# One lot of contractions per step: moving half of a step's y-contraction to the beginning of the next step in a convolution, scan and experts kernel

## The chip, the cores and the metric

One NeuronCore of a Trainium2 chip. The metric is the device time of one launch in microseconds; where several executions are compared, their median is taken. Engine names are those of the profile: PE is the TensorE (matmuls), PEld its weight loads, DVE the VectorE, ACT the ScalarE, POOL the GpSimd, SP the SyncE, which issues most of the DMAs.

## What is computed

Two layers on an input of 8 images, 128 channels, 64 x 64 pixels: a deformable 3 x 3 convolution, then a selective scan over the 4,096 pixels of each image as tokens, then a mixture of eight experts with the best two chosen. The scan is what matters here:

```python
deltaA = jnp.exp(jnp.einsum('bld,dn->bldn', delta, A))
deltaB = jnp.einsum('bld,bln->bldn', delta, Bv)

def step(state, inp):
    dA_i, dB_i, x_i, C_i = inp
    state = dA_i * state + dB_i * x_i[:, None, :]
    y = jnp.einsum('bdn,bn->bd', state, C_i)
    return (state, y)
```

`d` and `n` both run over 256, so each image has a state of 256 x 256 numbers, and each of the 4,096 steps multiplies it by the exponentials, adds an outer product and contracts it with `C`.

## The kernel before

**The steps.** All eight images advance together. One step takes a token of each. A state lies with `n` on the 128 partitions, in two halves `h`, and `d` along the row. The eight images are four pairs, `PAIRS = ((0, 2), (1, 3), (5, 7), (4, 6))`. Pairs 0 to 2 have their states in SBUF (`ht`), pair 3 in PSUM (`ud`). One step does, for each pair p:

- `product(j, c, lo, p)` (line 999): exponentials `et` times state, into a buffer. For pairs 0 to 2 it runs on POOL, into `mt[(3 * j + p) % 4]` (four buffers for three pairs), and for pair 3 on DVE, into `md[j % 2]`.
- `unit(c, lo, pairs)` (line 982): outer products on PE, for pairs 0 to 2 into `up`, which is one PSUM tile that the three pairs use in turn, for pair 3 into `ud`.
- `add(j, p)` (line 1006): DVE adds product and outer product into the new state, `ht[p]` or `ud`.
- `contract(j, c, lo, pairs)` (line 1013): PE multiplies the *product* by `C` and accumulates in `yp`, 16 matmuls for two pairs. (The outer product's share of y is added later, through `qt`.) Each matmul fills 32 of the array's columns, and four neighbours of the order fill all 128. It reads `mt` or `md`, so that buffer can't be written again before it is done.

Two steps are a chunk `c`. Their exponentials are made a chunk ahead: `decay` (line 952) makes one group of logarithms on PE in one of three PSUM banks, and ACT takes the exponential into the other of two `et` buffers. A chunk has 19 such groups.

**The order.** The program of every engine is written out by hand in `scan_block`: a step has 12 slots, and what is issued at a slot stands there. At slot 0 a decay, the contraction of pairs (1, 2) of the step before and `product` 2; at slot 3 `unit` of pairs 0 and 3 and `add` 0; at 5 `add` 3; at 6 `unit` 1 and, in the first step of a chunk, the contraction of pairs (0, 3) of this very step; at 7 `add` 1; at 8 the contraction of (0, 3) in the second step of a chunk; at 9 `unit` 2; at 11 `add` 2. `product` 0 and 1 of a step stand ahead of its slots; that of pair 3 is issued at slot 9 or 11 of the step before. Decays stand at the head of nearly every slot.

The rest (gathers and convolution of the block ahead, its projections, and the experts of the block behind) is fed into the slots by a planner, `Work.step` (line 482). It keeps a load for PE and DVE, which `cost` raises with each piece (5 for a contraction of two pairs, 2 for `unit`, 1 for `decay` on PE; 6 for a large DVE operation). Each slot takes `RATE` off the load, and a thread may issue its next piece only if both loads are below `ROOM`.

Sixteen steps are a block, 32 blocks one body of the loop, and the loop runs eight times. Before it the images are normalised and their table of gather addresses is made (the first 1.8 ms).

Of the kernel before, what the change touches and what calls it, by code (L numbers as in the profile page):

```python
# [46 lines left out]
CH = 2  # L47
# [19 lines left out]


RATE = (3.2, 3.2)
ROOM = (7.0, 9.0)  # L70

PACE = 0.8
AHEAD = 2.0
# [3 lines left out]
def kernel(  # L77
# [392 lines left out]
    def cost(pe=0, dve=0):  # L470
        load[0] += pe
        load[1] += dve
        paced[0] += pe * paced[1]

    class Work:
# [3 lines left out]
        def add(self, gen, at=0):  # L479
            self.threads.append([gen, at])  # L480

        def step(self, slot):
# [5 lines left out]
            for t in list(self.threads):  # L488
                if t[1] <= slot and all(x < r for x, r in zip(load, ROOM)):
                    n = next(t[0], None)  # L490
# [433 lines left out]
    def load_r(k, c):  # L924
        assert ("rows", k) in there
        nc.sync.dma_start(
            out=rt[c % 2],
            in_=rz[k].rearrange("q x -> (q x)")[: KR * NCH * RROW].rearrange(
                "(p c x) -> p c x", p=KR, c=NCH
            )[:, c, :],  # L930
        )

    def load_u(k, c):
        assert ("delta", k) in there and ("b", k) in there
        for p in range(QI // 2):
            nc.sync.dma_start(
                out=uu[c % 2][32 * p : 32 * p + 9].rearrange("r w b l n -> r (w b) (l n)"),
                in_=pr[k].rearrange("i j p w b l n -> p (i j) (w b) (l n)")[
                    p, :, :, CH * DIN * c : CH * DIN * c + CH * DIN
                ],  # L940
            )
# [10 lines left out]
    def decay(c, g):  # L952

        ps = banks.pop(0)
        rv = rt[c % 2].rearrange("p (q g t) -> p q g t", q=GD, t=CT)
        if g < NG - 1:
            fs, n, d0 = 1, GD, P * (g % 2) + GD * (g // 2)
        else:
            fs, n, d0 = 2, P - NA * GD, NA * GD
        m = n * CT  # L960
        for h in range(NH):
            for f in range(fs):
                nc.tensor.matmul(  # L963
                    ps[:, m * (NH * f + h) : m * (NH * f + h + 1)].rearrange(
                        "p (q t) -> p q t", q=n
                    ),
                    alhs[:KR, g + f, P * h : P * h + P], rv[:, :n, g + f, :],
                    start=True, stop=True,
                )
        ec = et[c % 2].rearrange("p l b h d -> p h (l b) d")  # L970
        for f in range(fs):
            nc.scalar.activation(  # L972
                ec[:, :, :, P * f + d0 : P * f + d0 + n],
                ps[:, m * f * NH : m * (f + 1) * NH].rearrange(
                    "p (h d t) -> p h t d", h=NH, d=n
                ),
                AF.Exp,
            )
        banks.append(ps)
        cost(1)  # L980

    def unit(c, lo, pairs):

        for h in range(NH):
            for p in pairs:
                for r, b in enumerate(PAIRS[p]):
                    rows = slice(32 * (b // 2), 32 * (b // 2) + 32)
                    nc.tensor.matmul(  # L988
                        (up if p < QP else ud)[:, r, h],
                        uu[c % 2][rows, 0, b % 2, lo, P * h : P * h + P],  # L990
                        uu[c % 2][rows, 1, b % 2, lo, :], start=True, stop=True,
                    )
        cost(2)

    def buf(j, p):

        return mt[(QP * j + p) % 4] if p < QP else md[j % 2]

    def product(j, c, lo, p):
        (nc.gpsimd if p < QP else nc.vector).tensor_tensor(  # L1000
            buf(j, p), et[c % 2][:, lo, PAIRS[p][0] : PAIRS[p][1] + 1 : 2],
            ht[p] if p < QP else ud, ALU.mult,
        )
        cost(0, 0 if p < QP else 6)
# [8 lines left out]
    def contract(j, c, lo, pairs):  # L1013
        l = j % BL
        for h in range(NH):
            for r in range(2):
                for p in pairs:
                    b = PAIRS[p][r]
                    s0 = 32 * (CH * (QI * h + b) + lo) + 31 - (BL * (b % 2) + l)
                    nc.tensor.matmul(  # L1020
                        yp[32 * (b // 2) : 32 * (b // 2) + 32, :DIN],
                        zc[c % 2].rearrange("p s x -> p (s x)")[:, s0 : s0 + 32],
                        buf(j, p)[:, r, h, :],
                        start=(l == 0 and h == 0 and b % 2 == 0),
                        stop=(l == BL - 1 and h == NH - 1 and b % 2 == 1),
                    )
        cost(5)

    def after(k, c, n):

        return ((k + (c + n) // NCH) % 2, (c + n) % NCH)

    last = []

    def scan_block(s, work):

        k = s % 2
        for c in range(NCH):
            for lo in range(CH):
                j0 = CH * c + lo  # L1040
                j = BL * s + j0
                if lo == 0:
                    load_u(*after(k, c, 1))
                    load_r(*after(k, c, 2))
                for p in range(2):
                    product(j, c, lo, p)
                for sl in range(NSLOT):
                    x = NSLOT * lo + sl

                    g = x * NG // (CH * NSLOT - 3)  # L1050
                    if g < NG and (x == 0 or g > (x - 1) * NG // (CH * NSLOT - 3)):
                        decay((c + 1) % NCH, g)
                    nxt = (j + 1, c + (lo + 1) // CH, (lo + 1) % CH)
                    if sl == 0:
                        if last:
                            contract(*last.pop())
                        product(j, c, lo, 2)
                    elif sl == 3:
                        unit(c, lo, (0, 3))
                        add(j, 0)  # L1060
                    elif sl == 5:
                        add(j, 3)
                    elif sl == 6:
                        unit(c, lo, (1,))
                        if lo + 1 < CH:
                            contract(j, c, lo, (0, 3))
                    elif sl == 7:
                        add(j, 1)
                        if lo == 0:
                            copy_c(*after(k, c, 1))  # L1070
                    elif sl == 8 and lo + 1 == CH:

                        contract(j, c, lo, (0, 3))
                    elif sl == 9:
                        if lo + 1 < CH:
                            product(*nxt, 3)
                        unit(c, lo, (2,))
                    elif sl == 11:
                        add(j, 2)
                        if lo + 1 == CH:  # L1080
                            product(*nxt, 3)
                        last.append((j, c, lo, (1, 2)))
                    work(NSLOT * j0 + sl)

    def run(gen):
        for _ in gen:
            pass
        while later:
            run(later.pop(0))

    for b0 in range(0, NB, QI):

        run(conv(b0, 0, 0))
        run(project(0))
        run(conv(b0, BL, 1))
        for p in range(QP):
            nc.vector.memset(ht[p], 0.0)
        nc.vector.memset(ud, 0.0)
        load_r(0, 0)
        load_r(0, 1)  # L1100
        load_u(0, 0)
        copy_c(0, 0)
        for g in range(NG):
            decay(0, g)
        product(0, 0, 0, 3)
        with tc.For_i(0, NBLOCK * BL, BODY * BL) as i0:
            with tc.manual_schedule():
                work = Work()
                load[:] = 0.0, 0.0
                paced[:] = 0.0, 0.0  # L1110
                for s in range(BODY):
                    work.add(project(1 - s % 2))
                    work.add(conv(b0, i0 + BL * (s + 2), (s + 2) % 4), CONV_AT - LOADS)
                    scan_block(s, work.step)
                    assert not [t for t in work.threads]

                    work.threads.insert(
                        0, [behind(b0, i0 + BL * s, s % 2, s % 4), 2]
                    )
                contract(*last.pop())  # L1120
                run(work.threads[0][0])


# [41 lines left out]
```

## Time and profile before

| | |
|---|---|
| median of 3 runs | 38,419.15 us (38,351.94 to 38,429.86) |
| the profiled execution's own time | 37,966.97 us |
| its span, first to last instruction | 37,965.3 us |
| granted TensorE clock, mean | 0.963 |
| loop, first to last product on POOL | 1,777 to 37,929 us |

The parts of a step that the change touches, from the groups of instructions (all lie inside the loop):

| what | engine, count | mean of one |
|---|---|---|
| contraction, L1020, from `mt` | PE, 98,304 | 395 ns |
| contraction, L1020, from `md` | PE, 32,768 | 407 ns |
| decay, L963 | PE, 81,960 | 254 ns |
| outer product into `up`, L988 | PE, 49,152 | 274 ns |
| exponential, L972 | ACT, 40,980 | 519 ns |
| product of pairs 0 to 2, L1000 | POOL, 12,288 | 2,367 ns |
| add into `ht`, L1008 | DVE, 12,288 | 1,218 ns |

Matmuls in different columns of the array run side by side, so a contraction of 16 matmuls takes not 16 x 0.4 us but about 1 us. The busy shares of the page are means over the whole loop. No engine is full, so the reader has to go by waits: who stood still, and for whom.

### The profile page before, as it was taken

The page shows a single profiled execution, that of the slowest core. Times are in us where ns is not written, and L with a number is a line of the kernel's source. Part 1 is how long each engine was busy: PE and PEld are TensorE (multiplying, and loading weights), DVE is VectorE, ACT ScalarE, POOL GpSimd, SP SyncE. Part 2 cuts the span into 40 slices and gives each one's busy share as a digit, 9 for nine tenths or more (in the row PEclk, how much of TensorE's full clock was granted, in tenths as well). Part 3 has the DMA queues.
Part 4 walks back from the last instruction along what each step waited for, and adds up shares of the span by engine and source line. Part 5 has one row for each costly group of instructions (what it writes and reads, how often), then busy time and mean ns, then how long its engine had stood idle before and what let it go on. Part 6 is the DMA issues. An engine that isn't in the chain of part 4 may idle for free. (4 is left out here: it accounts for less than half of the span.)

```text
span 37965.3 us, 852122 instructions
## 1 busy us (share of the span) xinstructions
PE 31439.9 (83%) x324270; PEld 17736.9 (47%) x324270; DVE 27307.6 (72%) x35860; ACT 24040.0 (63%) x62725; POOL 31045.4 (82%) x14691
## 2 busy tenths in 40 slices
PE   3488888888888888888888888888888888888888
PEld 1144444444444444444444444444444444444444
DVE  1277777777777777777777777777777777777777
ACT  0166666666666666666666666666666666666666
POOL 0188888888888888888888888888888888888888
PEclk7799999999999999999999999999999999999999
DMA  3333333333333333333333333333333333333333
GB/s 88 76 103 103 104 105 103 103 106 105 105 102 105 105 103 105 103 104 104 105 102 104 106 105 105 101 106 105 105 104 104 104 103 105 105 103 103 105 105 100
DMA packets 4799916, 3906.86 MB, mean 103 GB/s; under 512 B 3351550, under 2 KB 4378967, under 8 KB 4536023
## 3 DMA queue, kind: packets, MB, share of 16 engines
q1 hardware_dynamic: 4529962, 3182.00, 30.2%
q0 software_dynamic: 185760, 608.85, 5.9%
q10 hardware_dynamic: 80072, 61.51, 0.6%
q8 instruction: 2532, 41.48, 0.5%
q14 instruction: 1590, 13.02, 0.1%
HBM read 3268.71 MB, written 582.10 MB: 101 GB/s over the span
## 5 line engine op out<-in xcount | busy, mean ns | idle before, releaser
L1000 POOL TENSOR_TENSOR mt<-et,ht 128x1024 f32<-128x1024 f32 x12288 | 28725.1, 2367 | 4748.9 <-ACT et L972 3456.5
L972 ACT ACTIVATE et<-bank 128x448 f32<-128x448 f32 (+1 forms) x40980 | 19926.5, 519 | 10802.0 <-PE bank L963 10474.1
L1008 DVE TENSOR_TENSOR ht<-mt,up 128x1024 f32<-128x1024 f32 x12288 | 14968.0, 1218 | 8812.8 <-PE ud L988 5603.9
L963 PE MATMUL bank<-rt,alhs 126*128 126x224 bf16 (+1 forms) x81960 | 12579.9, 254 | 2341.6 <-ACT et L972 2056.9
L963 PEld LDWEIGHTS <-alhs 126*128 126x128 bf16 x81960 | 6874.8, 99 | 7549.5 <-issue 6746.3
L1020 PE MATMUL yp<-mt,zc 128*32 128x256 f32 x98304 | 9099.6, 395 | 0.0
L988 PE MATMUL up<-uu 32*128 32x256 bf16 x49152 | 4993.7, 274 | 1969.9 <-DVE ht L1008 1899.2
L1010 DVE TENSOR_TENSOR ud<-md,ud 128x1024 f32<-128x1024 f32 x4096 | 5004.4, 1222 | 0.0
L1000 DVE TENSOR_TENSOR md<-et,ud 128x1024 f32<-128x1024 f32 x4097 | 4975.1, 1214 | 23.7 <-ACT et L972 23.7
L1020 PEld LDWEIGHTS yp<-mt,zc 128*32 128x32 f32 x98304 | 3411.5, 111 | 2805.6 <-issue 1378.5
L1020 PE MATMUL yp<-md,zc 128*32 128x256 f32 x32768 | 4664.2, 407 | 0.0
L988 PEld LDWEIGHTS <-uu 32*128 32x128 bf16 x65536 | 1786.7, 92 | 5060.7 <-issue 4445.9
L611 PE MATMUL bank<-ident,w 128*128 128x128 f32 x18576 | 3142.5, 292 | 341.4 <-ACT et L972 216.0
L601 ACT ACTIVATE w<-g,rec 128x128 f32<-128x128 f32 x9288 | 3196.2, 404 | 127.2 <-DMA rec<-recs 114.6
L611 PEld LDWEIGHTS bank<-ident,w 128*128 128x128 f32 x18576 | 2429.5, 191 | 1136.1 <-ACT et L972 538.2
L578 POOL DMA_INDIRECT g<-table,rec x2322 | 2261.6, 974 | 500.6 <-issue 228.0
L988 PE MATMUL ud<-uu 32*128 32x256 bf16 x16384 | 1604.4, 272 | 361.5 <-DVE md L1000 342.8
L1020 PEld LDWEIGHTS yp<-md,zc 128*32 128x32 f32 x32768 | 1691.0, 113 | 0.0
L896 ACT ACTIVATE se<-bank,gate 128x128 f32<-128x128 f32 x2048 | 696.2, 367 | 540.2 <-PE bank L889 487.2
L301 POOL MEMSET xpad<- 128x66 f32 x8 | 1.2, 153 | 1232.7 <-POOLq L268 1232.6
L554 PE MATMUL bank<-wconv_sb,vt 128*128 128x128 f32 x4644 | 905.5, 295 | 0.0
L554 PE MATMUL bank<-ident,se 128*128 128x128 f32 x4096 | 820.7, 305 | 0.0
(200 smaller groups left out, 16358.4 us busy)
## 6 DMA issues: line engine op xcount, KB each, us to landing
rt<-rz SPq DMA_DIRECT2D x2050, 1102.5 KB
uu<-pr SPq DMA_DIRECT2D x8196, 36.0 KB
pr<-dpt SPq DMA_DIRECT2D x3084, 48.0 KB
pr<-bpt SPq DMA_DIRECT2D x3084, 48.0 KB
rz<-dst SPq DMA_DIRECT2D x6939, 21.0 KB
g<-table,rec POOLq DMA_INDIRECT x2322, 3.5
rec<-recs SPq DMA_DIRECT2D x2064, 2.8 KB
table<-xtok SPq DMA_DIRECT2D x256, 128.0 KB
```

The costliest lines, as they stand in the source:

```text
L554: nc.tensor.matmul(ps_out, lhs, rhs, start=(i == 0), stop=(i == n - 1))
L578: nc.gpsimd.indirect_dma_start(out=g, out_offset=None, in_=table, in_offset=bass.IndirectOffsetOnAxis(ap=rec.bitcast(I32)[:, j : j + 1], a ...
L601: nc.scalar.activation(ws[j][:, P * q : P * q + P], g[:, P * q : P * q + P], AF.Copy, scale=rec[:, c0 : c0 + 1],)
L611: nc.tensor.matmul(wk[:, :P], w[:, P * q : P * q + P], ident, start=(q == 0), stop=(q == 3),)
L896: nc.scalar.activation(se[:, ex, :], wk[:, P * j : P * j + P], AF.Copy, scale=gate[:, ex : ex + 1],)
L963: nc.tensor.matmul(ps[:, m * (NH * f + h) : m * (NH * f + h + 1)].rearrange("p (q t) -> p q t", q=n), alhs[:KR, g + f, P * h : P * h + P], ...
L972: nc.scalar.activation(ec[:, :, :, P * f + d0 : P * f + d0 + n], ps[:, m * f * NH : m * (f + 1) * NH].rearrange("p (h d t) -> p h t d", h= ...
L988: nc.tensor.matmul((up if p < QP else ud)[:, r, h], uu[c % 2][rows, 0, b % 2, lo, P * h : P * h + P], uu[c % 2][rows, 1, b % 2, lo, :], st ...
L1000: (nc.gpsimd if p < QP else nc.vector).tensor_tensor(buf(j, p), et[c % 2][:, lo, PAIRS[p][0] : PAIRS[p][1] + 1 : 2], ht[p] if p < QP else ...
L1008: nc.vector.tensor_tensor(ht[p], buf(j, p), up, ALU.add)
L1010: nc.vector.tensor_tensor(ud, buf(j, p), ud, ALU.add)
L1020: nc.tensor.matmul(yp[32 * (b // 2) : 32 * (b // 2) + 32, :DIN], zc[c % 2].rearrange("p s x -> p (s x)")[:, s0 : s0 + 32], buf(j, p)[:, r, ...
```

## The change

The contraction of pairs (0, 3) is no longer issued in its own step. It is kept in `last` with that of (1, 2), and both are issued in one lot in the next step, ahead of slot 0 and its decay. They stand behind that step's `product` 0 and ahead of its `product` 1. The latter writes the `mt` buffer that the contraction of pair 0 reads: `(3 * (j + 1) + 1) % 4` equals `(3 * j) % 4`. `ROOM` for PE goes from 7 to 9.

```diff
-ROOM = (7.0, 9.0)
+ROOM = (9.0, 9.0)
...
-                for p in range(2):
-                    product(j, c, lo, p)
+                product(j, c, lo, 0)
+                if last:
+                    for what in last.pop():
+                        contract(*what)
+                product(j, c, lo, 1)
...
                     if sl == 0:
-                        if last:
-                            contract(*last.pop())
                         product(j, c, lo, 2)
...
                     elif sl == 6:
                         unit(c, lo, (1,))
-                        if lo + 1 < CH:
-                            contract(j, c, lo, (0, 3))
...
-                    elif sl == 8 and lo + 1 == CH:
-
-                        contract(j, c, lo, (0, 3))
...
                         if lo + 1 == CH:
                             product(*nxt, 3)
-                        last.append((j, c, lo, (1, 2)))
+                        last.append([(j, c, lo, (0, 3)), (j, c, lo, (1, 2))])
...
-                contract(*last.pop())
+                for what in last.pop():
+                    contract(*what)
```

## The prediction

> **What bounds the kernel now.** First the page, part 1: is one engine full?
>
> ```profile
> PE 31439.9 (83%) x324270; PEld 17736.9 (47%) x324270; DVE 27307.6 (72%) x35860; ACT 24040.0 (63%) x62725; POOL 31045.4 (82%) x14691
> ```
>
> None is. PE and POOL are both near 82%, so the waits have to say who holds whom. The view of waits (engine and line, what it waited for: us in total, times, longest):
>
> ```profile
> ACT et L972 <- PE bank L963: 10474.1, 10831, 14.0
> ...
> DVE ht L1008 <- PE ud L988: 5603.9, 2797, 15.4
> ...
> POOL mt L1000 <- ACT et L972: 3456.5, 1606, 34.5
> DVE ht L1008 <- PE up L988: 2476.6, 3095, 2.7
> PE bank L963 <- ACT et L972: 2056.9, 5295, 1.1
> PE up L988 <- DVE ht L1008: 1899.2, 2718, 1.8
> ...
> POOL mt L1000 <- PE yp L1020: 687.8, 598, 2.9
> ```
>
> POOL, ACT and DVE wait for each other only through PE: ACT for decay matmuls, DVE for outer products (`unit`), and POOL for ACT's exponentials, once per pair of steps. PE's own waits are small and of two kinds: a decay that needs a free bank (ACT), and a `unit` that needs `up` free (the `add` on DVE). So PE's stream in its written order sets the pace, with a DVE or ACT leg now and then. The chain of waits near the end (start us, us, what) shows it, with a contraction (L1020) on the path:
>
> ```profile
> 36003.61 0.35 PE bank L963 x2
> 36003.96 0.32 PE up L988 x4
> 36004.29 1.00 PE yp L1020 x16
> 36005.29 0.31 PE bank L963 x2
> 36005.60 0.02 issue
> 36005.62 0.55 ACT et L972
> ...
> 36007.48 0.71 PE bank L611 x4
> 36008.19 0.19 PE bank L963 x2
> 36008.38 1.00 PE yp L1020 x16
> 36009.38 0.64 PE bank L611 x4
> ```
>
> The first is the contraction of pairs (0, 3), right behind `unit` 1, with the next decay and ACT behind it. The second is that of (1, 2).
>
> **The step as a timetable.** From the starts and ends in the timeline, averaged over all pairs of steps (an even step, then an odd one; 2,048 pairs; POOL's first product starts at 1,777 us and its last ends at 37,929, so a pair takes 36,152 / 2,048 = 17.65 us). PE's marks are the outer products u03 (slot 3), u1 (slot 6), u2 (slot 9):
>
> - u03 to u1: 2.58 us even, 2.02 odd. u1 waits for `add` 0.
> - u1 to u2, with the (0, 3) contraction inside: 3.04 even, 2.65 odd. u2 waits for `add` 1. In 25% of even and 34% of odd steps it starts within 0.1 us of that add's end; on average 0.83 and 0.39 us after it.
> - u2 to the next u03, with the (1, 2) contraction inside: 4.16 from an even step, 3.20 from an odd one.
>
> PE's idle time within the last stretch, per pair: waits right at u03 0.12 (odd) + 0.31 (even) = 0.43 us; at decays and work matmuls 0.12 + 0.17 + 0.07 + 0.04 = 0.40 us. At the decays between u03 and u1 another 0.49 + 0.24 = 0.73 us.
>
> [...] from the last contraction matmul to the next decay 0.312 us start to start, against 0.21 between rounds of four within the contraction. [...]
>
> **The change, part by part.**
>
> 1. *PE's work.* The same 32 matmuls a step, no DMA moved, no queue of SP passed. Start to start, the (0, 3) contraction in its old place costs 0.198 (from `unit`) + 0.692 + 0.312 = 1.20 us. With it gone, `unit` to decay is 0.200, so the stretch u1 to u2 loses 1.00 us. In the lot it adds 0.692 + 0.213 = 0.905 us. [...] 0.10 us a step, 0.20 a pair of steps, 0.4 ms (1%) if nothing else moved.
>
> 2. *u1 to u2.* u2 can't come 1.00 us sooner, as it waits for `add` 1, and neither `unit` 1 nor that add moves. Step by step, the smaller of 1.00 us and what u2 now has behind `add` 1: 0.58 us even, 0.34 odd. Gain 0.92 us a pair; the other 1.08 us turn into PE waiting for DVE.
>
> 3. *u2 to u03.* Plus 2 x 0.905 = 1.81 us. The waits at u03 (0.43) go, since DVE then has 0.9 us more. Of the 0.40 us at decays and work I let a quarter go (0.10): the bounds are all of it, and, on the other side, up to 0.5 more, because in a lot of 2 us without a decay ACT empties its banks (0.55 us each) and afterwards has three or four decays to take before u03, faster than it takes them. Now one contraction stands between decay 0 and decay 1 of the step and gives ACT that time; then none does. The nearest row for this is PE's 2,057 us of waits for a bank, 1.0 us a pair; I take half as its worst.
>
>    Sum: -0.92 + 1.81 - 0.43 - 0.10 = +0.36 us a pair.
>
> 4. *POOL.* `product` 1 of the next step writes the `mt` buffer that pair 0 of this step used, so it now waits for the lot's first half; behind it on POOL stand `product` 2 and the gathers. From an odd step to an even one the lot comes early (the (1, 2) contraction now begins 0.84 us before `product` 1; later by 0.05 us or nothing). From even to odd the (1, 2) contraction begins on average 0.72 us after `product` 1 starts; the lot, without the decay ahead of it and with u2 0.58 sooner, some 0.9 us before that, so its first half releases `product` 1 about 1.1 us late on average, in about two thirds of the steps. `product` 2, which waits there for (1, 2) already, is late by some 0.7 us. What hides it: `add` 1 of an odd step starts 4.2 us after its product's end (2.1 at the fifth percentile) and `add` 2 3.8 us after; and POOL's next even step starts 10.05 us after the odd one, while its three products end at 7.5. I cost it at nothing; without that cover it is up to 1.1 us a pair.
>
> 5. *ROOM and the planner.* The lot adds 10 to PE's load at one slot: 10 + 1 - 3.2 = 7.8 and what is left over, which the old bound of 7 would hold up and 9 mostly doesn't. Work at slot 0 may slip to slot 1, and slots 6 and 8 had room before. I cost it at 0, within 0.1 us either way.
>
> 6. *Other buffers.* `md` and `zc` keep two buffers and are read earlier in the step than they are rewritten (slot 9 and slot 7); `yp`'s readers in `behind` gain time. Nothing.
>
> The sum is 2,048 x 0.36 = 740 us on a profiled execution of 37,967 us (span 37,965, 2 us around it). The median of the runs shown is 38,419, 1.2% above; I add the 740 there: 39,160 us, +1.9%.
>
> **Rivals.** With x for the waits of PE that the lot absorbs per pair, the change is 1.81 - 0.92 - x = 0.89 - x; the forecast has x = 0.53.
>
> - *The lot absorbs more (faster).* ACT, freed of the hole in mid-step, keeps the banks free: all 0.83 us between u2 and u03 go and half of the 0.73 us at the decays before u1, x = 1.20, -0.31 us a pair, 37,790 us. It decides from x = 0.89. For it: ACT's 10.5 ms behind decays, some of it behind the mid-step contraction as in the chain. Against: ACT is busy 63%, and it is PE and DVE that are late.
> - *POOL becomes the bound (slower yet).* Even to odd, a quarter of the steps have the (1, 2) contraction 1.7 us or more behind `product` 1; there it is 1.9 us late, near the 2.5 us that POOL has at the end of the odd step, from which gathers of 0.97 us are still taken. If half of 1.1 us comes through: +0.36 + 0.55 = 0.91 us a pair, 40,280 us. Against it: the means leave over a microsecond.
> - *A draw.* x near 0.89, or the planner moves work into the gap at u2 and fills it: 38,420 us. The planner counts slots and load, not waits, so it doesn't see the gap.
>
> **How the numbers follow.** Forecast 0.56, with its own range from x = 0.83 (+0.06 us) to the worst for ACT and the planner (0.36 + 0.5 + 0.1 = +0.96): 38,540 to 40,390. Faster rival 0.24, POOL 0.14, draw 0.06. A change below 0.2% can't be told from none here. So faster 0.24, same 0.06, slower 0.70. The range for 8 in 10 reaches from the faster rival's time, 37,800, leaving half of it out, to 40,100, which leaves out the slower half of POOL's.
>
> **What would show it.** Right: runs of 32 matmuls at L1020; PE's waits for `ht` and `ud` at L988 up by about a millisecond or two; u1 to u2 near 2.4 us; POOL's waits for L1020 up from 688 us to some 2,000 and more, with `add` 1 not waiting for POOL. Wrong: PE's waits for `et` falling by more than those for `ht` rise (then it is faster), or DVE's waits for `mt` at L1008 (494 us now) growing to milliseconds (then POOL bounds).

## The result, and the profile after

| | before | after |
|---|---|---|
| median | 38,424.51 us (4 runs) | 41,408.93 us (4 runs) |
| ratio | | 1.0784, 95% interval 1.0765 to 1.0803 |
| profiled span | 37,965.3 us | 41,380.2 us |
| mean granted TensorE clock of the profiled execution | 0.963 | 0.908 |
| one pair of steps, first to last product on POOL over 2,048 | 17.65 us | 19.32 us |

The change costs 7.8%. One of the four executions before took 61,190 us, and the ratio, which compares fast runs, leaves it out. The profiled execution before is 1.2% below the median (more on that at the end), so the profiles differ by 1.67 us a pair, 3.4 ms, where the medians differ by 3.0.

Part 1 of the page after: no engine has become the bound, all shares fell, and PE's busy time *rose* by 2.1 ms with the same 324,270 matmuls.

```profile
PE 33502.6 (81%) x324270; PEld 18941.0 (46%) x324270; DVE 27267.1 (66%) x35860; ACT 23798.5 (58%) x62725; POOL 31076.3 (75%) x14691
```

The waits after (engine and line, what it waited for: us in total, times, longest):

```profile
ACT et L972 <- PE bank L963: 15036.5, 8943, 13.2
DVE ht L1008 <- PE ud L988: 10256.3, 3832, 15.5
...
POOL mt L1000 <- PE yp L1020: 4423.3, 2378, 4.3
PE up L988 <- DVE ht L1008: 2855.9, 2936, 1.9
PE bank L963 <- ACT et L972: 2514.2, 6566, 4.4
POOL mt L1000 <- ACT et L972: 2438.6, 1470, 33.6
...
DVE ht L1008 <- PE up L988: 1554.8, 2683, 1.1
...
DVE ht L1008 <- POOL mt L1000: 140.3, 33, 5.0
```

ACT waits 4.6 ms longer for decays; DVE waits 4.7 ms longer for outer products into `ud` and 0.9 less for those into `up`. POOL waits for the contraction as forecast (688 us before), yet DVE waits for POOL's products only 140 us. So PE itself is late. The chain of waits after (start us, us, what) has the reason in two lines that should be alike:

```profile
36525.04 0.39 PE up L988 x4
36525.43 0.64 PE bank L554 x4
36526.08 1.86 PE yp L1020 x32
...
36534.50 0.48 PE bank L963 x2
36534.98 2.86 PE yp L1020 x32
```

The same lot of 32 matmuls takes 1.86 us once and 2.86 us once. Over all 4,096 lots the span from the first to the last start is 1.56 us at the median, 3.01 us at the 90th percentile. The groups of instructions of after (busy us, mean ns) show it in the mean, which was 395 and 407 ns before:

```profile
L1020 PE MATMUL yp<-mt,zc 128*32 128x256 f32 x98304 | 9948.9, 453 | 0.0
...
L1020 PE MATMUL yp<-md,zc 128*32 128x256 f32 x32768 | 5464.1, 463 | 0.0
```

The view by windows shows when. Four stretches of 3.41 us in a row, after; the columns are the stretch, its length, busy us of PE, PEld, DVE, ACT and POOL with instruction counts, granted clock (PEclk), DMA share and GB/s:

```profile
20006.27:20009.68 3.41, 3.06 (x42) 1.56 (x30) 3.13 (x13) 2.17 (x5) 3.28 (x2) 1.00 0.02 5
20009.68:20013.09 3.41, 0.99 (x12) 0.74 (x12) 3.38 (x3) 2.39 (x8) 1.90 (x2) 1.00 0.09 22
20013.09:20016.50 3.41, 3.39 (x32) 1.51 (x35) 2.35 (x2) 0.00 (x0) 2.69 (x2) 0.50 0.33 77
20016.50:20019.92 3.42, 2.84 (x30) 1.73 (x23) 1.46 (x2) 2.30 (x7) 3.42 (x2) 1.00 0.70 281
```

In the second stretch PE works 0.99 us of 3.41. In the third its clock is 0.50, it is busy throughout, and ACT runs nothing. What PE did around it, in the timeline (start us, us, engine line operation, and the idle time ahead with its releaser):

```profile
20010.85 0.39 PE L988 MATMUL up<-uu 32*128 32x256 bf16 x4 [1.07 <-DVE ht L1008]
20011.17 0.37 PE L963 MATMUL bank<-rt,alhs 126*128 126x224 bf16 x2
20011.38 0.28 PE L632 MATMUL bank<-ident,tn 128*128 128x128 f32 x1
20011.49 0.26 PE L963 MATMUL bank<-rt,alhs 126*128 126x32 bf16 x4
20013.11 0.61 PE L988 MATMUL up<-uu 32*128 32x256 bf16 x4 [1.37 <-DVE ht L1008]
20013.65 0.64 PE L1020 MATMUL yp<-mt,zc 128*32 128x256 f32 x1
...
20014.08 0.63 PE L1020 MATMUL yp<-mt,zc 128*32 128x256 f32 x1
...
20015.36 1.59 PE L1020 MATMUL yp<-mt,zc 128*32 128x256 f32 x16
```

The two L988 rows are u1 and u2, each after more than a microsecond of waiting for DVE's add; only the last decays and one transpose stand between them, where the (0, 3) contraction used to be as well. Then the lot comes, its rounds of four matmuls 0.43 us apart instead of 0.21.

Of the 1,997 times at half clock in the two traces, all but the last of each trace lasted 3,413 ns or a multiple of it, within 1 ns. Cut into pieces of that length (the "windows" of the expectations below), the loop before and after (first to last product on POOL) gives the following, with PE's busy share from the spans of its matmuls, and pieces at full clock alone:

| PE busy in the piece | before: pieces, of them next at half clock | after: the same |
|---|---|---|
| below 0.50 | 166, 166 | 1,167, 1,167 |
| 0.50 to 0.75 | 2,045, 239 | 1,374, 363 |
| 0.75 and above | 7,875, 0 | 7,120, 36 |

The way back took more here. Of 138 pieces at half clock in the two traces in which PE was busy for less than 0.80, one was followed by full clock; of 1,836 above 0.95, all but 32 were. (At half clock the same work keeps PE busy for longer: the lots below spread their starts over 3.01 us instead of 1.56.) The kernel before drops to half clock too, though less often. Two stretches of it in a row, the first with PE busy for 0.54 of the time:

```profile
20031.38:20034.79 3.41, 1.85 (x20) 0.90 (x19) 3.23 (x6) 1.58 (x5) 3.29 (x3) 1.00 0.71 279
20034.79:20038.20 3.41, 3.41 (x25) 1.95 (x24) 3.34 (x4) 0.51 (x2) 3.12 (x2) 0.50 0.27 62
```

So the time that the loop spends at half clock rose from 1.75 to 6.62 ms (from 1,750 us on). Most of it meets the lots: in the stretches from u2 to u03 it rose from 0.43 to 5.87 ms. Of the 4,096 lots, 2,573 lie wholly in full clock, with 1.56 us from the first to the last start, and 611 wholly in half clock, with 3.01 us; the rest lie across a change. The drops aren't spread evenly: of 1,568 changes from full to half clock, 1,465 begin in steps 0, 2, 3, 4, 6 and 7 of a block.

### The profile page after: what moved, and what is told of

Its sections match the earlier page's. It is cut to its first block, busy times and chain, and to the rows that moved or that the text cites. A ratio compares the mean times of both kernels' runs of the same rounds, so it can differ in the third digit from the quotient of the medians.

```text
span 41380.2 us, 852138 instructions
## 1 busy us (share of the span) xinstructions
PE 33502.6 (81%) x324270; PEld 18941.0 (46%) x324270; DVE 27267.1 (66%) x35860; ACT 23798.5 (58%) x62725; POOL 31076.3 (75%) x14691
## 5 line engine op out<-in xcount | busy, mean ns | idle before, releaser
L963 PE MATMUL bank<-rt,alhs 126*128 126x224 bf16 (+1 forms) x81960 | 12931.5, 257 | 3103.3 <-ACT et L972 2514.2
L1020 PE MATMUL yp<-mt,zc 128*32 128x256 f32 x98304 | 9948.9, 453 | 0.0
L988 PE MATMUL up<-uu 32*128 32x256 bf16 x49152 | 4995.4, 280 | 3166.6 <-DVE ht L1008 2855.9
L1020 PEld LDWEIGHTS yp<-mt,zc 128*32 128x32 f32 x98304 | 4344.2, 129 | 4103.5 <-issue 2355.9
L1020 PE MATMUL yp<-md,zc 128*32 128x256 f32 x32768 | 5464.1, 463 | 0.0
L988 PEld LDWEIGHTS <-uu 32*128 32x128 bf16 x65536 | 1821.7, 92 | 5147.0 <-issue 4959.9
L611 PEld LDWEIGHTS bank<-ident,w 128*128 128x128 f32 x18576 | 2535.8, 198 | 584.2 <-ACT et L972 256.8
L1020 PEld LDWEIGHTS yp<-md,zc 128*32 128x32 f32 x32768 | 1852.4, 124 | 0.0
L988 PE MATMUL ud<-uu 32*128 32x256 bf16 x16384 | 1601.5, 273 | 1.1 <-DVE md L1000 0.6
```

The source lines that it names most:

```text
L611: nc.tensor.matmul(wk[:, :P], w[:, P * q : P * q + P], ident, start=(q == 0), stop=(q == 3),)
L963: nc.tensor.matmul(ps[:, m * (NH * f + h) : m * (NH * f + h + 1)].rearrange("p (q t) -> p q t", q=n), alhs[:KR, g + f, P * h : P * h + P], ...
L988: nc.tensor.matmul((up if p < QP else ud)[:, r, h], uu[c % 2][rows, 0, b % 2, lo, P * h : P * h + P], uu[c % 2][rows, 1, b % 2, lo, :], st ...
L1020: nc.tensor.matmul(yp[32 * (b // 2) : 32 * (b // 2) + 32, :DIN], zc[c % 2].rearrange("p s x -> p (s x)")[:, s0 : s0 + 32], buf(j, p)[:, r, ...
```

## The experiments

Three theories. *Clock*: without its mid-step contraction the stretch before u2 falls below half busy, and the lot behind it runs at half clock. *ACT*: only the order counts; the lot starves ACT, and PE waits for it afterwards. *POOL*: the new wait of `product` 1 is the bound. All ratios are against the kernel before, on the same chip. That kernel ran at a clock of 0.963 to 0.966 there, but at 0.954 to 0.956 on the chip of the four runs from "lot, filler of 8" to "before, (1, 2) late in step 2".

| run | ratio, interval | clock | half-clock ms in the loop |
|---|---|---|---|
| ROOM alone | 0.9998, 0.9990 to 1.0007 | 0.965 | 1.65 |
| lot, five `mt` | 1.0936, 1.0918 to 1.0954 | 0.904 | 6.97 |
| lot, filler of 16 | 1.0842, 1.0824 to 1.0860 | 0.962 | 2.12 |
| before without (0, 3) | 1.0343, 1.0325 to 1.0360 | 0.853 | 10.50 |
| lot, filler of 8 | 1.0653, 1.0636 to 1.0669 | 0.942 | 3.73 |
| before, (1, 2) at slot 5 | 0.9899, 0.9884 to 0.9914 | 0.961 | 1.90 |
| before, filler in step 2 | 1.0018, 1.0011 to 1.0025 | 0.963 | 1.84 |
| before, (1, 2) late in step 2 | 1.0146, 1.0131 to 1.0162 | 0.937 | 3.85 |
| lot, once more | 1.0915, 1.0896 to 1.0933 | 0.906 | 6.75 |
| lot, filler in five steps | 1.0821, 1.0803 to 1.0839 | 0.924 | 5.20 |
| before, five `mt` | 1.0123, 1.0106 to 1.0140 | 0.954 | 2.53 |
| lot, filler of 16, once more | 1.0848, 1.0830 to 1.0866 | 0.960 | 2.25 |

**ROOM alone.**

```diff
-ROOM = (7.0, 9.0)
+ROOM = (9.0, 9.0)
```

> The kernel before with ROOM (9, 9) alone. If the planner's new bound (other places for the convolution and expert work) is what costs time, a good part of the 3.0 ms shows: above 39.5 ms. If it is the place of the contractions, it stays within 0.4 ms of 38.4 ms, and the time at half clock within the loop stays near the 1.7 ms of before.

37,948.6 against 37,961.95 us. In the kernel before the planner's bound does nothing. In the changed kernel it wasn't put back, but there the bound and the lot together moved only some 1,000 matmuls of the planner's work from the stretch between u2 and u03 to the others.

**A fifth `mt` buffer in the changed kernel.**

```diff
-    mt = several(4, [P, 2, NH, DIN], FP, "mt")
+    mt = several(5, [P, 2, NH, DIN], FP, "mt")
...
-        return mt[(QP * j + p) % 4] if p < QP else md[j % 2]
+        return mt[(QP * j + p) % 5] if p < QP else md[j % 2]
```

> The changed kernel with five mt buffers instead of four (room made by three gather buffers instead of four and two shared small tiles), so that product 1 no longer waits for the lot. POOL's waits for L1020 fall from 4.4 ms to under 1 ms. Theory POOL (the new wait became the bound): the time falls by 1.5 ms or more, to below 39.9 ms. Theory clock and theory ACT (the lot starves ACT): it stays within 0.4 ms of 41.4 ms.

41,516.6 us. In its view of waits what POOL waits for by the contraction is gone, and the time is what it was:

```profile
POOL mt L1000 <- PE yp L1020: 303.4, 348, 1.8
```

Theory POOL falls.

**The (0, 3) contraction left out of the kernel before.**

```diff
-                        if lo + 1 < CH:
-                            contract(j, c, lo, (0, 3))
...
-                    elif sl == 8 and lo + 1 == CH:
-
-                        contract(j, c, lo, (0, 3))
...
-                        start=(l == 0 and h == 0 and b % 2 == 0),
+                        start=(l == 0 and h == 0),
```

> The kernel before with the contraction of pairs (0, 3) left out (y then lacks the images of those pairs; 65,536 matmuls, 1.2 us of PE a step, are gone and no lot is made). Theory clock: the same stretch before u2 goes quiet, the half-clock time in the loop rises from 1.7 ms to 4 ms or more, and the time falls little or not at all: 37.5 to 39 ms. Theories of order alone (ACT starved by the lot, POOL's wait): no lot and no wait, so the 0.92 us a pair that u2 gains remain: 36.5 ms or less, with the clock as before.

39,249.3 us: with 65,536 matmuls less and no lot, the kernel is 3.4% *slower* than before. Its own groups and its mean clock:

```profile
L1020 PE MATMUL yp<-mt,zc 128*32 128x256 f32 x65536 | 5525.2, 466 | 0.0
```

```profile
core 0: 39236.4 us, clock 0.853
```

The contraction that is left stands where it did and takes 466 ns a matmul instead of 395. Two neighbouring stretches of this run, in the view by windows:

```profile
20035.18:20038.59 3.41, 0.73 (x12) 0.23 (x10) 2.36 (x2) 0.51 (x3) 3.41 (x3) 0.99 0.91 332
20038.59:20042.00 3.41, 2.72 (x12) 2.26 (x12) 0.00 (x0) 2.63 (x7) 3.41 (x2) 0.50 0.06 21
```

The same picture as after: PE busy 0.73 us of 3.41, then half clock. All 1,055 full-clock pieces below half busy were followed by half clock here. The stretch from u2 to u03 holds the same 139,074 matmuls as before, yet PE is busy in it for 8.0 us a pair instead of 6.7. Neither theory of order (ACT, POOL) gives a slower kernel here; 39.25 is even a little above the 39.0 that theory clock allowed.

**A filler in the old place, in the changed kernel.** 16 matmuls on the products of pairs 0 and 3, with 32 columns of zeros as weights.

```diff
+    def filler(j, c):
+        if j % BL == 0:
+            return
+        for h in range(NH):
+            for r in range(2):
+                for p in (0, 3):
+                    b = PAIRS[p][r]
+                    nc.tensor.matmul(
+                        yp[32 * (b // 2) : 32 * (b // 2) + 32, :DIN],
+                        zc[c % 2][:, NH * QI * CH, :],
+                        buf(j, p)[:, r, h, :], start=False, stop=False,
+                    )
...
                         unit(c, lo, (1,))
+                        if lo + 1 < CH:
+                            filler(j, c)
+                    elif sl == 8 and lo + 1 == CH:
+                        filler(j, c)
```

> The changed kernel with 16 extra matmuls where the (0, 3) contraction used to stand (weights all zero, added into yp; not in the first step of a block). They add about 1.0 us of PE work a step. Theory clock [...]: the half-clock time in the loop falls from 6.6 ms to under 2.5 ms, the lot's mean length from 2.0 to about 1.6 us, and the time does not rise: 40.0 to 41.4 ms in spite of the added work. Theory ACT or any theory in which only the order of work counts: the stretch from u1 to u2 grows back by 0.4 us a step or so with nothing in return, so the time rises by 1.5 ms or more, to 42.9 ms and above.

41,142.01 us, then beside the changed kernel itself on one chip:

> The changed kernel once more, unchanged, so that the runs with a filler stand beside it on one chip: ratio 1.07 to 1.09.

> The changed kernel with 16 filler matmuls in every step but the first of a block, once more, beside the changed kernel on the same chip. Theory clock: clock about 0.96, and the time at or a little below the changed kernel's (0.985 to 1.000 of it).

41,427.3 us without and 41,161.83 us with the filler. 61,440 matmuls more, and 0.6% faster. The clock is back, and so is the length of the contraction's matmuls, in the groups of the last run:

```profile
L1020 PE MATMUL yp<-mt,zc 128*32 128x256 f32 x98304 | 8196.1, 391 | 0.0
...
L1020 PE MATMUL yp<-md,zc 128*32 128x256 f32 x32768 | 4499.2, 395 | 0.0
```

These two runs also part the loss. The mean lengths of the stretches between PE's marks, in us per pair of steps (even and odd added):

| | u03 to u1 | u1 to u2 | u2 to u03 | pair |
|---|---|---|---|---|
| before | 4.60 | 5.69 | 7.36 | 17.65 |
| lot | 4.23 | 4.89 | 10.24 | 19.34 |
| lot with filler | 4.37 | 5.68 | 9.17 | 19.21 |

The filler puts u1 to u2 back to its old length and takes 1.07 us out of the stretch in which the lot stands, without a change to its work. A rival reading is that u2, coming later, leaves PE less to wait for in that stretch; but PE stands idle there for 0.54 us a pair without the filler and 0.56 with it. So PE does the same 203,586 matmuls 1.07 us a pair faster. The time at half clock within the stretch fell from 5.99 to 1.14 ms. As the lots took about twice as long at half clock (3.01 us and 1.56), half of that difference would be the loss, by estimate 1.18 us a pair. This is the price of the half clock there. What is left of that stretch is +1.81 us against before. If the 0.79 us that the filler adds from u1 to u2 are taken off the 1.56 us by which its pair is longer than before, the order alone would cost some 0.8 us a pair and the clock the other 0.9 of 1.69. That split is an estimate, since the filler isn't free of effects on its neighbours. The two waits that grew most in the changed kernel don't go with the clock: with the filler ACT still waits 14.8 ms for decays, and DVE 9.1 ms for outer products into `ud`.

**Half the filler.** `for h in range(1)` in place of `range(NH)`.

> The changed kernel with a filler of 8 matmuls (weights zero) at the old place of the (0, 3) contraction, half of that in the run with 16. Start to start it costs some 0.57 us a step where 16 cost 1.00. If the clock was a large part of the loss, half the filler is enough or nearly: half-clock time under 3.5 ms, and the time lies below both the changed kernel and the one with 16: 40.0 to 40.8 ms. If the clock costs nothing, the time lies between the kernel with 16 and the changed kernel: at 41.1 ms or above.

40,933.9 us, below both others but above the expected 40.8, with 3.73 ms at half clock where under 3.5 was expected. Against the changed kernel's 1.0784, on a chip with the same time before, 1.0653.

**The filler where the drops are.** In steps 1, 3, 5, 7 and 15 alone.

```diff
-        if j % BL == 0:
+        if j % BL not in (1, 3, 5, 7, 15):
             return
```

> The changed kernel with the filler of 16 matmuls only in steps 1, 3, 5, 7 and 15 of a block, ahead of whose ends the changed kernel's half-clock windows begin (1,465 of 1,568 in steps 0, 2, 3, 4, 6 and 7). Theory clock: half-clock time between 2 and 4 ms, and as only 5 steps of 16 carry the added work, the time lies below the changed kernel by 0.6 ms or more, and below the runs with filler in every step. If the clock costs nothing, it lies at the changed kernel's time or above.

41,055.47 us: less than the changed kernel by 0.37 ms, not by 0.6, and half-clock time 5.20 ms, above the range. The drops of steps 0 and 6 are gone (244 and 242 to none), 148 more appear in step 1, and those of steps 4 and 7 stay. The time does lie below the runs with filler in every step, as expected. Filling one window may shorten the steps and set the next windows elsewhere; that was not tried by itself.

**The same in the kernel before.** Most of the 407 drops in its profile begin in steps 2 and 3. First 16 filler matmuls behind u03 of step 2; then no added work, but the (1, 2) contraction moved there.

```diff
                         add(j, 0)
+                        if j % BL == 2:
+                            filler(j, c)
```

> The kernel before with 16 filler matmuls (weights zero) in one step of sixteen, behind u03 of step 2, where most of its own half-clock windows begin (249 of 407 begin in steps 2 and 3). Theory clock: those fall below 60, half-clock time from 1.7 ms to about 1.0, and the time falls by 0.1 to 0.4 ms although work is added: ratio 0.990 to 0.998. If the clock costs nothing: 256 times up to 1.0 us more, ratio 1.000 to 1.007.

38,497.82 against 38,425.58 us: missed, a little slower. Drops in steps 2 and 3 went from the 249 of the profile before, on another chip, to 156, those in step 5 rose from 30 to 115. The clock was better than that of the kernel before on this chip, 0.963 against 0.955, so here a higher clock did not quite pay for the added matmuls.

```diff
                     if sl == 0:
-                        if last:
-                            contract(*last.pop())
-                        product(j, c, lo, 2)
+                        if j % BL != 2:
+                            if last:
+                                contract(*last.pop())
+                            product(j, c, lo, 2)
...
+                    elif sl == 4 and j % BL == 2:
+                        contract(*last.pop())
+                        product(j, c, lo, 2)
```

> The kernel before with the (1, 2) contraction moved from slot 0 to slot 4 in step 2 of each block only (product 2 with it, as it rewrites a buffer that the contraction reads). No work added. Theory clock: the quiet window of step 2 is filled, half-clock windows in steps 2 and 3 fall from 249 to under 80, ratio 0.985 to 0.997. If the clock costs nothing, 0.999 to 1.004.

39,001.06 us: missed, and in the other direction. 250 drops now begin in step 2 itself, and 83 in step 3. The contraction's old place at slot 0 is what was emptied, so it seems that one window was filled at the cost of the one ahead of it. The longer time comes with a lower clock, 0.937 against 0.955 of the kernel before on that chip. But `product` 2 was moved too, and POOL waits 1.3 ms for the contraction where it waited 0.7 in the profile before, so the clock isn't the only thing that differs.

**The other contraction moved in every step.**

```diff
-                        if last:
+                        if last and j % BL == 0:
                             contract(*last.pop())
...
                     elif sl == 5:
                         add(j, 3)
+                        if last:
+                            contract(*last.pop())
```

> The kernel before with the other contraction moved: that of (1, 2) of the step before stands at slot 5, between u03 and u1, instead of slot 0 (five mt buffers so that product 2 needn't wait; at the first step of a block it stays at slot 0). Timetable: u03 to u1 holds 0.63 and 0.51 us of PE waits that it can use, so grows by about 0.4 and 0.5; u2 to u03 shrinks by up to 1.0 from an even step and little from an odd one, where DVE sets it. Sum near nothing: 37.5 to 38.4 ms with the clock as before. If the stretch from u2 to u03 then goes quiet, the half-clock time rises above 4 ms and the time above 38.4 ms.

> The kernel before with five mt buffers (and three gather buffers, two shared tiles) and nothing else, the control for the run with (1, 2) at slot 5. POOL's 0.7 ms of waits for L1020 go, but no engine waited for POOL there: ratio 0.997 to 1.003. If it is 0.990, the buffers and not the place of the contraction made that run faster.

38,056.72 us, 1.0% faster than before on its chip. The timetable held: u03 to u1 +1.51 us, u1 to u2 -0.35, u2 to u03 -1.12 a pair, sum +0.04 against the profile before. As no stretch of the timetable gives a gain, it goes with the clock, 0.961 against 0.955. The control, the kernel before with five `mt` buffers and nothing else, took 38,414.85 us. That is slower by 1.2%, at clock 0.954 against 0.964, and a miss, though only POOL had waited for the buffer (0.7 ms). It is also the time of the unchanged kernel on the other chip, 38,425.58 us, and whether the edit or something outside it made the clock lower was not tried. So a gain of 1.0% is within what the clock does for reasons not known here. That this kernel beats the one before is shown on that chip only: on the two chips where before runs at 0.964 it takes 37.95 ms, less than this.

## Why the prediction was wrong

The direction was right, and the size was 1.9% where 7.8% came; the range ended at 40,100 us. By its steps:

1. *PE's work.* Right at full clock: a lot's first to last start 1.56 us where 0.692 + 0.213 + 0.692 = 1.60 was taken. But the term is a time at the clock granted before, and the mean lot took 2.00 us after. What makes the 0.312 us from a contraction to a decay was not shown: from an outer product to a contraction, where the shape of the matmuls changes too, it is 0.198.
2. *u1 to u2.* Near: -0.80 us against -0.92, and the rest turned into PE waiting for DVE (1,899 to 2,856 us at L988). **This is the step that failed**: "the other 1.08 us turn into PE waiting for DVE" priced that wait as time alone. The wait made the stretch quiet, and all 1,167 pieces of the trace after in which PE was busy for less than half were followed by 3.4 us or more at half clock, which is when the lot runs. The run without (0, 3), at ratio 1.0343 and clock 0.853, shows that quiet alone, with no lot, is enough to make the kernel slower.
3. *u2 to u03.* Mis-sized: +1.28 us a pair forecast, +2.85 measured. 1.07 of the difference is the clock (lot with and without filler). The other half microsecond is smaller errors. The 0.43 us of waits at u03 did go, but 0.18 of them, ahead of the third matmul of u03, lie behind the mark, and so in the stretch from u03 to u1. The waits at decays and work rose from 0.39 to 0.54 us instead of losing a quarter. And at the filler's clock two lots made PE busy for 1.89 us more, not 1.81. The stretch u03 to u1, taken as unchanged, gave 0.38 us back. From u2 to the next u1 PE's idle time fell by 0.50 us a pair (0.36 in the run with filler), so the term "absorbed", 0.53, was about right as a sum, though not in its parts.

   With the some 0.8 us a pair that the order alone costs by the estimate above, in place of 0.36, the forecast would have been some 40,000 us, just within its range. By this estimate it is the clock that took the result out of it.
4. *POOL.* Right: its waits rose to 4.4 ms, above the 2,000 and more forecast, and were hidden, as a fifth buffer shows.
5. *ROOM.* Right, nothing.
6. *Other buffers.* Nothing was seen that speaks against it.

The rival that the lot absorbs more failed: it decides from x = 0.89, and x was 0.5 at most. Rival POOL named a slower time for a reason that isn't there. No rival had the clock, though the page of the profile before gave it in its second part and the mean, 0.963, was in the table.

## What to carry to other kernels

As in the run without (0, 3), 3.4% slower with 65,536 matmuls less, idle time on PE can cost more than itself. Before work is taken out of a stretch where PE waits for another engine, count PE's busy share over 3.4 us there, and if it falls below a half, price what comes next at half clock, which is what followed 166 of 166 and 1,167 of 1,167 such pieces here. Work that seems to be in the way of a waiting engine may be what keeps the clock up, as the (0, 3) contraction did (0.963 to 0.966 with it, 0.853 without). A change of PE's order should be read with the granted clock beside every duration, before any theory of waits.

## What the runs showed of the hardware

- Leaving out 65,536 of 324,270 matmuls made the kernel 3.4% slower, at a mean clock of 0.853 instead of 0.963 to 0.966.
- Matmuls with weights of zero hold the clock up too: with them the changed kernel spent 2.25 instead of 6.75 ms of the loop at half clock.
- The kernel before runs in 37.95 ms at clock 0.964 to 0.965 on two chips and in 38.42 ms at 0.954 to 0.955 on another, each within 0.3%. Its profile in the table (0.963) goes with the first, its median of 38,424 us with the second. The changed kernel took 41,409 us in the result and 41,427 beside the first, so the change costs 7.8% or 9.2% by which of the two it is held against. Why chips differ in this was not tried.
